# A graph-network stack on TensorE: masks made further ahead, loads less far ahead, and the three-term features moved into the gates' operand tiles

## The chip, the cores and the metric

The kernel runs on one core of one Trainium2 chip. The metric is the device time of one execution in microseconds; the median of three runs is quoted. A profile is one further execution. The engines are TensorE (PE, with its weight loads PEld), VectorE (DVE), ScalarE (ACT), GpSimd (POOL) and SyncE (SP, which issues DMAs). Each engine takes its instructions in the order in which the program holds them.

## What is computed

There are N = 3327 nodes with 64 features each, and one adjacency matrix `adj` (3327 x 3327, float32, some 0.5% of it nonzero). Four layers follow each other, each on the layernorm of the running sum:

```
h = relu(layernorm(x)); x = x + layer(h, adj)
layer 0: two gated cells: m = adj @ (h @ W); gates r, z, n from m and h; h = relu((1-z)*n + z*h)
layer 1: mask = adj != 0; rank = cumsum(mask, axis=1); k = min(deg, 100); pos = rank - (deg - k)
         out = (mask * where(pos > 0, 0.5**(k - pos), 0)) @ (h @ weight) + bias
layer 2: w = adj*adj; three times: h = (w @ h) @ W.T + b
layer 3: two hops: h = tanh(concat(adj @ h, h) @ W)
```

So the adjacency is passed over eight times: twice plain, once with weights by rank (the nonzero entry counted from the end of a row gets a power of one half), three times with squared entries, and twice plain.

## The kernel before

**Tiles and passes.** The transposed, padded adjacency lies in HBM as 26 source blocks of 128 rows. The target nodes are cut into four chunks (`CH`, three of 2 x 384 columns and one of 2 x 512), and these into two groups (`GROUPS`): group 0 is chunks 0 and 1 (768 KB per tile), group 1 is chunks 2 and 3 (896 KB). A `Tile` is one source block for one group. It is loaded into one of 20 slots (`slots`, named adj in the profile) by SP (L368). A unit is (pass k, chunk c, tile): it multiplies the tile's columns of the chunk with the features `y[k]` of the source block and adds to the chunk's sum in PSUM (L561). Passes 0, 1, 6 and 7 are PLAIN, pass 2 is RANKED, passes 3, 4 and 5 are SQUARED.

**The order of units** is written out ahead: `alone(0, 0)`, then `joint(1, 0)`, `joint(0, 1)`, `joint(1, 2)` and so on to `alone(0, 7)`. In `joint(g, k)` each tile of group g serves pass k and pass k + 1, so that the matrix is loaded four and a half times rather than eight. There are 914 units. Units 250 to 313 are pass 2 of group 0, units 314 to 389 pass 2 of group 1, from unit 326 on in turn with units of pass 3.

**The ranked pass.** A unit of pass 2 needs the tile's mask (`Mask`), a bf16 0/1 tile of which half a slot, a room, holds one. `make_mask` puts two pieces, one per half of the columns, into the queue `pieces`. A piece is a compare on DVE (L426); the first piece also issues, on POOL, a DMA of one row of totals into the mask's last row (L431). `run` lets pieces out one by one as units pass (`mask_pieces`); units of pass 2 that belong to group 0 on both sides let none out. What a unit needs is forced out when it is expanded, three units ahead of its own matmuls. `expand` multiplies the mask by a triangular matrix on PE (L270) and turns the two PSUM banks into weights, on ACT (L476) or DVE (L474). Masks of the count (k = -1, in pass 0) are made in the same way without the totals row. For group 0's tiles of pass 2 the mask is made where pass 1 has used the tile (`early`).

**The planner.** For each unit i, `run` first loads tiles up to `LOAD` = 60 units ahead, as long as more than three free slots (`RESERVE`) remain in `dead`. Then it prepares: `prepare` makes masks and squares tiles in place (ACT L403, DVE L405). It goes strictly in the order of the units and stops at the first unit that lies further ahead than its kind allows: 6 units for all kinds but RANKED, 44 for RANKED. So a unit of pass 3 that is more than 6 ahead holds up all masks behind it. Free slots and rooms are handed out first in, first out.

**Tasks between passes.** When a chunk's sum is complete, a generator (`after_0` and so on) evacuates it and computes the next features. Each `yield` names a time; the planner counts that down by the units it puts out and then puts out the next part of the task. If a unit needs features that aren't there, `finish` puts out all that is left of the task. Thus a `yield` decides where a task's instructions stand in each engine's queue. `layernorm_relu` (L761 to L781) computes mean and variance on DVE, the power -0.5 on POOL (L776) and the scaled result on DVE (L780). `gru` (L796 to L840) evacuates into `both` (the gates' operand tiles, two half-filled planes per chunk), computes the gates and, in the first cell, writes relu halves back with ACT (L837) and DVE (L838); L722 then turns these into node rows on PE. `in_three` (L844 to L866) splits the features of pass 2 into three bf16 terms, in one slot per group, and sends the terms' last rows to `lasty` by POOL (L865). The four first layernorms (`before_0`) are put out by a loop at the end, which advances chunks in the order 0, 0, 1, 0, 1, 2, 1, 2, 3, 2, 3, 3.

Of the kernel before, what the change touches and what calls it, by code (L numbers as in the profile page):

```python
# [46 lines left out]
NB = 13  # L47
# [5 lines left out]
NC = 4  # L53
# [18 lines left out]
KIND = [PLAIN, PLAIN, RANKED, SQUARED, SQUARED, SQUARED, PLAIN, PLAIN]  # L72
COUNT = -1
NBUF = 20
LOAD = 60
PREPARE = {COUNT: 6, PLAIN: 6, RANKED: 44, SQUARED: 6}
EXPAND = 3
RESERVE = 3
SPECIAL = None
# [11 lines left out]
def upper(n):  # L91
    return slice(n * D, (n + 1) * D)
# [3 lines left out]
def kernel(  # L96
# [383 lines left out]
            t.mask.free()  # L480
        return wide.bitcast(BF16)

    ranks_left = set(sources_of(*GROUPS[0]))
    counts = {}
    squared = {}

# [46 lines left out]
    def propagate(k, c, t, rhs, first, last):  # L533
        if k == COUNT:
            count(t, first, last)
            return
        w = width(c)
        if first:
            sums[k, c] = [take(sums=True) for _ in range(2 if k == 7 and c == PARTS[1] else 1)]
            sums[k, c] = [sums[k, c][0], sums[k, c][-1]]  # L540
        acc = sums[k, c]
        if t is SPECIAL:
            for ch in range(NC):
                if ch != c:
                    finish(ch)
            terms = [[lasty[:, h, i, :] for h in range(2)] for i in range(3)]
            rhs = [rhs, rhs]
        else:
            s, b = divmod(t.q, NB)
            cs = chunk_of(b)  # L550
            if y[k][cs] is None:
                finish(cs)
            terms = [[yk[:, b - CH[cs][0], s, :]] * 2 for yk in (y[k][cs] if KIND[k] == RANKED else [y[k][cs]])]
            rhs = [rhs[:, h, :] for h in range(2)]
            if KIND[k] != RANKED:
                t.used()
            if (k, c, t) in squared:
                squared.pop((k, c, t)).free()
        for n, yq in enumerate(terms):
            for h in range(2):  # L560
                nc.tensor.matmul(acc[h][1][h * D:(h + 1) * D, :w], yq[h], rhs[h], start=first and n == 0,  # L561
                                 stop=last and n == len(terms) - 1)
        if KIND[k] == RANKED and c == NC - 1 and t is not SPECIAL and chunk_of(t.q % NB) in GROUPS[0]:
            ranks_left.discard(t.q)
            if not ranks_left:
                dead.append(parts[0])
        if t is not SPECIAL and t.early and t.mask is None:
            make_mask(t, RANKED)
        spend(STREAM_US * w / CWM * (0.75 if KIND[k] == RANKED else 1.0))
        if last:  # L570
            begin(c, after[k](c, sums.pop((k, c))))
            if KIND[k] == RANKED and c == NC - 1:
                dead.append(parts[1])

    units = []

# [38 lines left out]
    def joint(g, k, sweep, later, keep, lag=None):  # L615
# [45 lines left out]
        for c in (a, b):  # L661
            for t in own[1]:
                put(k + 1, c, t)
            if KIND[k + 1] == RANKED:
                units.append((k + 1, c, SPECIAL))

    def run():
        total = {}
        for k, c, t in units:
            total[k, c] = total.get((k, c), 0) + 1  # L670
        done = {}
        loaded, prepared, expanded = 0, 0, deque()
        for i, (k, c, t) in enumerate(units):
            while loaded < len(units) and loaded < i + LOAD:
                u = units[loaded][2]
                if u is not SPECIAL and u.slot is None:
                    if len(dead) <= RESERVE and loaded > i + EXPAND:
                        break
                    u.load()
                loaded += 1  # L680
            while prepared < loaded and prepared < i + PREPARE[KIND[units[prepared][0]] if units[prepared][0] != COUNT
                                                               else COUNT]:
                if prepared > i + PREPARE[PLAIN] and not spare and len(dead) <= RESERVE + 1:
                    break
                prepare(*units[prepared])
                prepared += 1
            while len(expanded) < min(EXPAND + 1, len(units) - i):
                assert prepared > i + len(expanded)
                expanded.append(expand(*units[i + len(expanded)]))
            if k != 2:  # L690
                mask_pieces(1 + len(pieces) // 6)
            elif not (c in GROUPS[0] and (t is SPECIAL or chunk_of(t.q % NB) in GROUPS[0])):
                mask_pieces(1)
            n = done[k, c] = done.get((k, c), 0) + 1
            propagate(k, c, t, expanded.popleft(), n == 1, n == total[k, c])
# [65 lines left out]
    def layernorm_relu(h, c, scale=None, pace=1.0, squares_on_scalar=False):  # L761
        n = 2 * blocks(c)
        v = groups(xchunk(c))
        st = work.tile([P, 4, 8], F32, name="st", bufs=4)
        xc = work.tile([P, 8, D], F32, name="t2")
        nc.vector.tensor_reduce(st[:, 0, :n], v, AX.X, ALU.add)
        nc.vector.tensor_scalar(st[:, 1, :n], st[:, 0, :n], 1.0 / D, None, op0=ALU.mult)
        nc.vector.tensor_tensor(xc[:, :n], v, st[:, 1, :n, None].to_broadcast([P, n, D]), ALU.subtract)
        yield 1.5 * pace
        if squares_on_scalar:  # L770
            nc.scalar.activation(groups(h), xc[:, :n], AF.Square)
        else:
            nc.vector.tensor_tensor(groups(h), xc[:, :n], xc[:, :n], ALU.mult)  # L773
        nc.vector.tensor_reduce(st[:, 2, :n], groups(h), AX.X, ALU.add)
        nc.vector.tensor_scalar(st[:, 2, :n], st[:, 2, :n], 1.0 / D, EPS, op0=ALU.mult, op1=ALU.add)  # L775
        nc.gpsimd.tensor_tensor(st[:, 3, :n], st[:, 2, :n], mhalf[:, :n], ALU.pow)  # L776
        yield 2.5 * pace
        if scale is not None:
            nc.vector.tensor_scalar(st[:, 3, :n], st[:, 3, :n], scale, None, op0=ALU.mult)
        nc.vector.scalar_tensor_tensor(groups(h), xc[:, :n], 0.0, st[:, 3, :n, None].to_broadcast([P, n, D]),  # L780
                                       op0=ALU.max, op1=ALU.mult)  # L781
# [14 lines left out]
    def gru(acc, c, bi, bh, cell, pace=1.0):  # L796

        w = width(c)
        evacuate_stacked(acc, c)
        yield 0.8 * pace  # L800
        at = dead.popleft()
        r, z, d = (slots[at].rearrange("p s w -> p (s w)")[:, i * CWM:i * CWM + w] for i in range(3))

        def gate(g):
            i, ps = take()
            for s in range(2):
                nc.tensor.matmul(ps[upper(1 - s), :w], cells[:, cell, s, g, :], both[c][:, s], start=True, stop=True)
            return i, ps

        for g, v in enumerate((r, z)):  # L810
            i, ps = gate(g)
            nc.scalar.activation(v, ps[:, :w], AF.Sigmoid, bias=bsum[:, cell, g:g + 1])
            give(i)
        nh = None if cell == 0 else gate(2)
        ni = gate(3)
        yield 1.0 * pace
        nc.vector.scalar_tensor_tensor(r, ahead[c] if nh is None else nh[1][:, :w], bcol[:, bh + 2:bh + 3], r,
                                       op0=ALU.add, op1=ALU.mult)
        nc.vector.tensor_tensor(r, r, ni[1][:, :w], ALU.add)
        give(ni[0])  # L820
        if nh is not None:
            give(nh[0])
        else:
            del ahead[c]
            if not any(ch in ahead for ch in GROUPS[c // 2]):
                rooms[c // 2].free()
        yield 1.0 * pace
        nc.scalar.activation(r, r, AF.Tanh, bias=bcol[:, bi + 2:bi + 3])
        yield 0.8 * pace
        for s in range(2):  # L830
            u = upper(1 - s)
            nc.vector.tensor_tensor(d[u], both[c][u, s], r[u], ALU.subtract)
        nc.vector.tensor_tensor(d, d, z, ALU.mult)
        nc.vector.tensor_tensor(d, d, r, ALU.add)  # L834
        yield 2.2 * pace
        if cell == 0:
            nc.scalar.activation(both[c][upper(1), 0], d[upper(1)], AF.Relu)  # L837
            nc.vector.tensor_scalar(both[c][upper(0), 1], d[upper(0)], 0.0, None, op0=ALU.max)  # L838
            yield 1.0 * pace
        return at, d  # L840

    parts = {}

    def in_three(h, c):  # L844

        g = c // 2
        if g not in parts:
            parts[g] = dead.popleft()
        n = blocks(c) * 2 * 3 * D
        first = 2 * 3 * D * blocks(GROUPS[g][0]) if c == GROUPS[g][1] else 0  # L850
        room = slots[parts[g]].bitcast(BF16).rearrange("p s w -> p (s w)")[:, first:first + n]
        room = room.rearrange("p (b s i d) -> p b s i d", s=2, i=3, d=D)
        terms = [room[:, :, :, i, :] for i in range(3)]
        for i in range(2):
# [167 lines left out]
```

## Time and profile before

| | us |
|---|---|
| median of 3 runs | 720.03 (719.84 to 720.97) |
| profiled execution | 723.89 |
| its span, first to last instruction | 722.1 |
| PE busy | 690.7 (96%) |
| DVE busy | 346.2 (48%) |
| ACT busy | 264.3 (37%) |
| POOL busy | 77.3 (11%) |
| mean granted clock of PE | 0.993 |
| HBM read | 199.45 MB, 277 GB/s over the span |

The profile is a record of each instruction's start and duration, with what ended the idle time before it. Its views are a page of totals; the busy time per stretch (one row per stretch, one column per engine); the waits (who waited for whom, in total); the chain that ended last; and the timeline, in which instructions of one kind are merged and the idle time before the first stands in brackets. Line numbers are those of the program. Buffers' numbers are left out of names, so that `adj` is any of the 20 slots. The ends of matmuls are modelled, so PE can show as busy where it waits a little between two starts.

### The profile page before, as it was taken

What the parts mean: (1) busy time and instruction counts of PE and PEld (TensorE: products, weight loads), DVE (VectorE), ACT (ScalarE), POOL (GpSimd) and SP (SyncE); (2) the same over time, 40 slices, a digit from 0 to 9 for tenths busy, and PEclk for the clock granted to TensorE, in tenths of its full rate; (3) what the DMA queues carried; (4) which work ended last, traced back from release to release, by engine and by line L of the source; (5) the groups of instructions that cost most, each with busy time, mean ns of one, the idle gap of its engine ahead of it and who ended that gap; (6) DMA issues with size and microseconds to landing.
All of it is one profiled execution on the core that took longest, in us unless ns stands there. A gap on an engine that the chain in (4) does not pass through costs nothing.

```text
span 722.1 us, 12647 instructions
## 1 busy us (share of the span) xinstructions
PE 690.7 (96%) x5128; PEld 347.6 (48%) x5128; DVE 346.2 (48%) x701; ACT 264.3 (37%) x402; POOL 77.3 (11%) x114
## 2 busy tenths in 40 slices
PE   4999899999999897989999999999999999999997
PEld 1645444565446585445534444334444444344464
DVE  6767636634987987638615101521063456005101
ACT  0104000302137665778899321850065700000101
POOL 3500000001380602112100000000010000000000
PEclk9999999999999999999999999999999999999999
DMA  9999994299595367562799829981997399927991
GB/s 349 401 385 406 405 391 145 63 375 374 181 315 210 114 225 237 184 227 97 260 336 386 314 88 397 405 319 40 366 382 263 111 382 406 406 110 250 400 402 44
DMA packets 68549, 201.31 MB, mean 279 GB/s; under 512 B 7228, under 2 KB 8228, under 8 KB 68492
## 3 DMA queue, kind: packets, MB, share of 16 engines
q1 hardware_dynamic: 65596, 199.46, 74.6%
q8 instruction: 40, 0.66, 0.4%
q10 hardware_dynamic: 720, 0.85, 0.3%
q0 software_dynamic: 2176, 0.20, 0.2%
q14 instruction: 17, 0.14, 0.0%
HBM read 199.45 MB, written 0.85 MB: 277 GB/s over the span
## 4 chain that ended last, share of the span: by engine, by line
PE 52%; ACT 4%; DMA 2%; DVE 1%; issue 1%; ACTq 0%
PE sum L561 48%; ACT adj L403 3%; PE temp L270 3%; DMA adj<-totals 1%; PE temp L722 1%; DVE adj L426 1%; DMA out<-xs 1%; DVE both L757 0%; ACT both L756 0%; DVE xs L955 0%; ACT t L701 0%; PE sum L270 0%; ACT t L952 0%; ACT e L476 0%; ACTq L957 0%
## 5 line engine op out<-in xcount | busy, mean ns | idle before, releaser
L561 PE MATMUL sum<-adj,y 128*64 128x384 f32 (+3 forms) x3016 | 535.2, 505 | 12.1 <-DVE y L773 8.4
L561 PEld LDWEIGHTS sum<-adj,y 128*64 128x64 f32 x3016 | 223.3, 138 | 267.5 <-issue 223.8
L403 ACT ACTIVATE adj<-adj 128x768 f32<-128x768 f32 (+1 forms) x173 | 141.9, 891 | 50.2 <-PE sum L561 24.8
L426 DVE TENSOR_SCALAR adj<-adj 128x768 bf16<-128x768 f32 (+3 forms) x208 | 115.6, 606 | 32.4 <-PE temp L496 28.5
L476 ACT ACTIVATE e<-temp,bitsb 128x384 int16<-128x384 f32 (+1 forms) x114 | 65.4, 607 | 29.2 <-PE temp L270 16.1
L561 PE MATMUL sum<-e,adj 128*64 128x384 bf16 (+1 forms) x624 | 73.2, 341 | 0.6 <-DVE e L474 0.6
L757 DVE COPY both<-sum 64x384 f32<-64x384 f32 (+3 forms) x17 | 9.7, 568 | 117.1 <-ACT both L756 116.0
L756 ACT COPY both<-sum 64x384 f32<-64x384 f32 (+3 forms) x17 | 8.1, 478 | 154.8 <-PE sum L561 149.2
L270 PE MATMUL temp<-adj,tri 128*64 128x384 bf16 (+1 forms) x334 | 52.7, 348 | 8.7 <-DMA adj<-totals 5.4
L405 DVE TENSOR_TENSOR adj<-adj 128x768 f32<-128x768 f32 (+1 forms) x35 | 33.6, 1008 | 50.1 <-DMA adj<-in_adjT 29.6
L776 POOL TENSOR_TENSOR st<-st,mhalf 128x6 f32<-128x6 f32 (+1 forms) x16 | 24.5, 1531 | 295.5 <-DVE st L775 295.5
L561 PEld LDWEIGHTS <-adj 128*64 128x64 bf16 x624 | 40.3, 110 | 18.8 <-issue 6.7
L431 POOL DMA_DIRECT2D adj<-totals x52 | 31.4, 605 | 139.8 <-DVE adj L834 74.4
L474 DVE TENSOR_SCALAR e<-temp 128x384 int16<-128x384 f32 (+1 forms) x53 | 31.8, 607 | 26.3 <-issue 11.3
L270 PEld LDWEIGHTS <-tri 128*64 128x64 bf16 x416 | 28.9, 111 | 30.2 <-issue 13.7
L751 DVE STREAM_TRANSPOSE both<-y 32x96 f32<-32x96 f32 (+1 forms) x128 | 35.6, 278 | 2.9
L703 DVE COPY t<-sum 128x384 f32<-128x384 f32 x8 | 4.4, 555 | 62.2 <-PE sum L561 62.2
L496 PE MATMUL temp<-adj,behind 128*64 128x384 bf16 x208 | 29.1, 342 | 0.8 <-DVE adj L426 0.7
L496 PEld LDWEIGHTS <-behind 128*64 128x64 bf16 x208 | 14.1, 112 | 20.8 <-issue 18.6
L701 ACT COPY t<-sum 128x384 f32<-128x384 f32 (+1 forms) x8 | 4.2, 529 | 53.9 <-PE sum L561 53.9
L918 DVE TENSOR_TENSOR y<-temp,brow 128x384 f32<-128x384 f32 (+1 forms) x8 | 4.7, 592 | 29.6 <-PE temp L270 29.6
L530 ACT ACTIVATE lastw<-adj,bitsb 128x768 int16<-128x768 f32 (+1 forms) x2 | 2.0, 984 | 45.8 <-DVE adj L528 45.8
(121 smaller groups left out, 336.7 us busy)
## 6 DMA issues: line engine op xcount, KB each, us to landing
adj<-in_adjT SPq DMA_DIRECT2D x130, 768.0 KB, 8.7
adj<-in_adjT SPq DMA_DIRECT2D x104, 896.0 KB, 12.5
xs<-in_x SPq DMA_DIRECT2D x1, 640.0 KB, 4.0
adj<-totals POOLq DMA_DIRECT2D x26, 3.0 KB, 4.6
adj<-totals POOLq DMA_DIRECT2D x26, 3.5 KB, 3.1
out<-xs ACTq DMA_DIRECT2D x2, 192.0 KB
out<-xs ACTq DMA_DIRECT2D x1, 256.0 KB, 6.4
stage<-in_weights SPq DMA_DIRECT2D x2, 112.0 KB, 13.3
```

The lines of the kernel that those rows point to most:

```text
L270: nc.tensor.matmul(out[hs], lhsT[:, hs], rhs, start=start, stop=stop)
L403: nc.scalar.activation(sq, v, AF.Square)
L405: nc.vector.tensor_tensor(sq, v, v, ALU.mult)
L426: nc.vector.tensor_scalar(t.mask.view[:rows, half], t.view()[:rows, half], 0.0, None, op0=ALU.not_equal)
L431: nc.gpsimd.dma_start(out=t.mask.view[P - 1:P], in_=totals[t.g][t.q:t.q + D + 1:D, :])
L474: nc.vector.tensor_scalar(wide[:, s], ps[:, :w], BITS, 0.0, op0=ALU.add, op1=ALU.max)
L476: nc.scalar.activation(wide[:, s], ps[:, :w], AF.Relu, bias=bitsb)
L496: nc.tensor.matmul(counts[c][1][s * D:(s + 1) * D, :w], behind[:, NQ - 1 - t.q:NQ - 1 - t.q + D], t.mask.view[:, s, t.cols(c)], start=firs ...
L561: nc.tensor.matmul(acc[h][1][h * D:(h + 1) * D, :w], yq[h], rhs[h], start=first and n == 0, stop=last and n == len(terms) - 1)
L751: nc.vector.transpose(to[at:at + 32, :, q], h[q * 32:(q + 1) * 32, :, s, f * 32:(f + 1) * 32])
L757: nc.vector.tensor_copy(both[c][upper(1), 1], acc[1][1][upper(1), :width(c)])
L776: nc.gpsimd.tensor_tensor(st[:, 3, :n], st[:, 2, :n], mhalf[:, :n], ALU.pow)
```

## The change

The planner gets three limits in the place of four. Loads go at most 44 units ahead instead of 60. All kinds are prepared 6 units ahead. Masks of pass 2 that aren't early are made by a loop of their own, up to 24 units ahead, and this loop passes over units of other kinds. Its condition on free slots is the old one. The features of pass 2 (`in_three`) lie in `both` instead of two slots, which therefore stay in `dead`. The layernorm gets one more `yield`, between the last DVE instruction of the variance and the power on POOL, and the one behind the power becomes 1.5 instead of 2.5. In `gru`, the first cell's relu on DVE stands ahead of the yield that it stood behind, and that yield becomes 2.4 instead of 2.2.

```diff
-LOAD = 60
-PREPARE = {COUNT: 6, PLAIN: 6, RANKED: 44, SQUARED: 6}
+LOAD = 44
+PREPARE = 6
+MASK = 24
...
-        if KIND[k] == RANKED and c == NC - 1 and t is not SPECIAL and chunk_of(t.q % NB) in GROUPS[0]:
-            ranks_left.discard(t.q)
-            if not ranks_left:
-                dead.append(parts[0])
...
-            if KIND[k] == RANKED and c == NC - 1:
-                dead.append(parts[1])
...
+    def is_masked(k, c, t):
+
+        return k != COUNT and KIND[k] == RANKED and t is not SPECIAL and not t.early and t.mask is None
+
...
-            while prepared < loaded and prepared < i + PREPARE[KIND[units[prepared][0]] if units[prepared][0] != COUNT
-                                                               else COUNT]:
-                if prepared > i + PREPARE[PLAIN] and not spare and len(dead) <= RESERVE + 1:
-                    break
+            while masked < min(loaded, i + MASK):
+                if is_masked(*units[masked]):
+                    if not spare and len(dead) <= RESERVE + 1:
+                        break
+                    make_mask(units[masked][2], RANKED)
+                masked += 1
+            while prepared < min(loaded, i + PREPARE):
                 prepare(*units[prepared])
                 prepared += 1
...
         nc.vector.tensor_scalar(st[:, 2, :n], st[:, 2, :n], 1.0 / D, EPS, op0=ALU.mult, op1=ALU.add)
+        yield 1.5 * pace
         nc.gpsimd.tensor_tensor(st[:, 3, :n], st[:, 2, :n], mhalf[:, :n], ALU.pow)
-        yield 2.5 * pace
+        yield 1.5 * pace
...
-        yield 2.2 * pace
+        if cell == 0:
+            nc.vector.tensor_scalar(both[c][upper(0), 1], d[upper(0)], 0.0, None, op0=ALU.max)
+        yield 2.4 * pace
         if cell == 0:
             nc.scalar.activation(both[c][upper(1), 0], d[upper(1)], AF.Relu)
-            nc.vector.tensor_scalar(both[c][upper(0), 1], d[upper(0)], 0.0, None, op0=ALU.max)
             yield 1.0 * pace
...
-        g = c // 2
-        if g not in parts:
-            parts[g] = dead.popleft()
-        n = blocks(c) * 2 * 3 * D
-        first = 2 * 3 * D * blocks(GROUPS[g][0]) if c == GROUPS[g][1] else 0
-        room = slots[parts[g]].bitcast(BF16).rearrange("p s w -> p (s w)")[:, first:first + n]
+        room = both[c].bitcast(BF16).rearrange("p s w -> p (s w)")[:, :blocks(c) * 2 * 3 * D]
```

## The prediction

> **What bounds the kernel now.** The first view is the busy time by stage. Columns: stretch and its length in us, then busy us (and instructions) of PE, PEld, DVE, ACT and POOL, granted clock, DMA share, GB/s.
>
> ```profile
> 0.00:20.00 20.00, 10.54 (x49) 4.27 (x50) 14.10 (x30) 1.28 (x1) 9.06 (x18) 1.00 0.93 354
> 230.00:250.00 20.00, 16.62 (x202) 12.27 (x197) 19.55 (x43) 14.14 (x30) 9.92 (x14) 1.00 0.34 118
> 267.00:285.00 18.00, 16.53 (x186) 12.30 (x181) 16.07 (x35) 11.59 (x19) 3.65 (x4) 1.00 0.88 295
> 285.00:295.00 10.00, 6.67 (x46) 3.12 (x46) 4.16 (x8) 3.98 (x6) 0.70 (x2) 0.83 0.09 22
> 317.00:327.00 10.00, 7.95 (x46) 3.16 (x44) 4.59 (x8) 5.08 (x8) 2.92 (x5) 0.83 0.42 146
> ```
>
> TensorE (PE) sets the pace: 690.7 of 722.1 us busy. The change adds and removes no matmul, so all it can win lies in some 31 us of PE idle time and in clock dips. That idle time sits at the start, in 230 to 250 (3.4 us, VectorE full), and round 288 and 320. Next, what PE waited for (total, times, longest):
>
> ```profile
> PE sum L561 <- DVE y L773: 8.4, 1, 8.4
> PE temp L270 <- DMA adj<-totals: 5.4, 2, 3.3
> PE sum L561 <- DMA adj<-in_adjT: 2.8, 5, 1.4
> PE temp L270 <- DVE e L474: 2.3, 3, 1.7
> PE sum L722 <- DVE both L838: 2.1, 1, 2.1
> ```
>
> All five are touched. Last, the timeline round the first and the longest wait for a mask's totals row:
>
> ```profile
> 7.37 0.56 DVE L780 SCALAR_TENSOR_TENSOR y<-t,st 128x384 f32<-128x384 f32 x1 [0.21 <-POOL st L776]
> 8.40 7.35 PE L561 MATMUL sum<-adj,y 128*64 128x384 f32 x32 [8.40 <-DVE y L773]
> ...
> 282.70 1.32 POOL L776 TENSOR_TENSOR st<-st,mhalf 128x6 f32<-128x6 f32 x1 [7.04 <-DVE st L775]
> 283.97 1.19 POOL L431 DMA_DIRECT2D adj<-totals  x2
> 285.13 1.15 DVE L426 TENSOR_SCALAR adj<-adj 127x896 bf16<-127x896 f32 x2
> 288.44 0.52 PE L270 MATMUL temp<-adj,tri 128*64 128x384 bf16 x4 [3.33 <-DMA adj<-totals]
> ```
>
> PE starts 0.47 us after L780 is done. At 288.44 it waits for a row whose DMA was issued at 283.97, behind a power on POOL (L776) that waited for DVE.
>
> **The Trainium skill.** (1) "TensorE: Matmul & The Clock Gate", What's actually happening: the clock is halved after an idle window of about 3.4 us, and windows run freely. The trace agrees in the loss: clock 0.83 in each ten-us stretch above is 1.7 us lost; but waits of 2.1 and 2.05 us were enough, so a window need not be wholly idle, and 1.65 us at 241 cost no clock. (2) "DMA: Bandwidth & Descriptors", Anatomy of one DMA: about 2 us fixed per DMA. Totals rows landed after 1.6 to 5.2 us here, 3.9 to 4.4 round 284. (3) "VectorE: DVE Perf Modes", the TRN2 errata section: 58 + FD/Accel cycles at 0.96 GHz; a mask half of 896 columns at 2x would take 527 ns. Ten back to back took 5.43 us: 0.54; between evictions 0.575. I use 0.56.
>
> **The change, step by step.** Sums are against the profiled execution, 723.89 us (span 722.1, 1.8 round it); the median of the runs is 720.03, 3.86 lower. I take the same microseconds off both. Program order is what the changed program's queues hold.
>
> *1. The layernorm's added yield, at the start.* The loop that interleaves the four first layernorms gives each three turns. With one yield more, all four L780 come after all four first halves on DVE. Before: first L780 at 7.37. Now DVE starts at 3.17 and does three halves of 2.65 (3.17 to 5.82 in the trace) and one of 3.1 (512 columns): 14.2. L780 0.56, then 0.47: PE starts at 15.2, 6.8 later. The cold 3.9 us are paid either way. Part is absorbed, since PE waited for tiles in this stage: from 8.40 to 20.79 it did 6 tiles of 1.29 (8 x 0.161, the pitch of 256 matmuls in 41.28 us), a count of 0.32 and 1.95 of cold loss: 2.4 us of waits. From 20.79 to 40.42, 19.63 for 10 tiles at 1.615 and transposes of 2.8: 0.7. From 40.42 to 57.14, 16.7 for 15.2 of work, at the tiles' pitch of 1.96: 1.5. So 6.8 - 4.6 = **+2.3** (ends +2, and +4.4 if only the first 2.4 is cover). The first chunk's transposes only change place.
>
> *2. The relu L838 ahead of the yield.* Before, it stood behind two mask halves and ended at 76.52; now right behind L834, at 72.7. PE's 2.1 goes. Next late: the count's mask, queued behind both L838, done at 77.1 while PE gets there at 75.5: 1.4 of waiting. The first matmul of pass 1 comes at 80.3 instead of 82.67: **-2.4**, of which 1.7 is the clock dip after the wait. Lower end -0.7 if the new wait still halves the clock.
>
> *3. No slot for the features.* Two of 20 slots stay free; the last six loads of pass 1's group 0 stand 2 to 4 units earlier in SP's queue. The 1.36 wait at 212 to 213.6 mostly goes: **-1.2** (0 to -1.4). The copies and subtractions are as many and as large.
>
> *4. Twelve mask halves leave 233 to 250.* In the program before, six masks of the second group were made here: 12 halves, 6.9 us busy of DVE's 19.55 in 20. They move to after 271. PE stands still for 20 - 16.62 = 3.4 us here, mostly for evictions L474. Without the masks DVE's remaining work (the layernorms and features of two chunks) lets an eviction through every 1.3 us, where PE needs one per two units, 1.6; some tenths stay at the start, where two come 2.3 apart. **-3.0** (-2 to -3.4). Nothing else is late there: ACT is busy 14.14 of 20.
>
> *5. They arrive in 267 to 295.* Chosen and uncertain. Pieces of a mask are not let out while group 0's own units run, so making masks at unit 291 doesn't spread them: in DVE's queue 15 more halves now stand between the pass-2 evacuation (267.43) and the eviction at 291.12. DVE's work there was 23.7 less 5.9 idle = 17.8; plus 15 x 0.56 = 26.2: the eviction at 293.6 at the earliest, +2.5. The totals row still goes out only when the power ahead of it is done; that waits for DVE, so 288.2 instead of 284, landing 1.6 to 4.4 later. PE's matmul of 288.44 then comes at 291.3 to 292.6. Its next 4.6 us were at half clock, 2.9 at full: +1.1 to +2.4 remain, and up to 1 more while DVE has four halves and two evictions (3.3) for PE's 3.39 per cycle. **+2.4** (0 to +5, with two clock dips). So the stall at 285 is not won; it turns into a wait for DVE. Queued behind the masks: evictions, so PE.
>
> *6. The wait at 320.* Four totals rows were issued together at 317.10, after an 8.4 us wait of POOL, and landed in 4.1 to 5.2. Their masks are now made 5 to 15 units earlier, in rooms that other masks have left (a unit takes 0.85 us of PE here): wait 2.05 and dip 1.7: **-3.75** (-2.05 if a dip remains). Next late there is PE itself, which is busy without a gap from 295 to 317.
>
> *7. Loads at most 44 ahead*: 0. Where it bites (pass 7, one to five units later) the three free slots are handed out in the same order, and SP waits for a slot's last reader, not for a unit. The cover is a full DMA queue (share 1.00 and 1.03 from 660 to 700); without it one tile, 2 us. The power's later place on POOL, behind two more totals rows: 0, since L780 comes a yield later too; otherwise 0.54 per row, in step 5's range.
>
> Sum: +2.3 - 2.4 - 1.2 - 3.0 + 2.4 - 3.75 = -5.65: profiled 718.2, median **714.4**.
>
> **Rivals.** *A, masks hidden:* step 5 wins its stall and dip, -5.0: sum -13.05, 707.0. For it: DVE idles 4.3 us between 285 and 291. Against: 26.2 us of DVE work don't fit into the 23.7 - 5.0 = 18.7 that PE would then need. *B, it doesn't do what it says at 320:* rows still late behind POOL's queue, step 6 is 0: 718.1. For it: rooms are reused at once, so a row waits for PE. Against: rooms' waits of 1.4 to 2.9 us, beside leads of 10 us and more. *C, slower, DVE full in 267 to 303:* none of the 15 halves falls in DVE's idle time, 8.6 us at 0.575 on top of the old stall, and one more dip, 1.7: step 5 is +10.3, sum +2.25, 722.3. It decides from a step 5 of +8.05, where the sum is 0. For it: 19.55 of 20 in step 4 shows what a full DVE does to PE. Against: PE's matmuls run three units ahead of their evicted masks.
>
> **How the numbers follow.** Forecast 0.57, A 0.10, B 0.18, C 0.15. The forecast's own range adds its steps' ends as independent: downward 0.3, 0.2, 0.4 and 2.4 give 2.5, upward 2.1, 1.7, 1.2, 1.0, 2.6 and 1.7 give 4.4: 711.9 to 718.8. The range 709.0 to 721.0 leaves out A and most of C. About 0.2% (1.4 us) is what a measurement tells from no change. Faster: 0.54 of the forecast, A, 0.12 of B, 0.76; same: 0.03, 0.05 of B and 0.03 of C, 0.11; slower: 0.01 of B and 0.12 of C, 0.13.
>
> **What would show it.** 1: PE's first matmul at 15.2, pass 0's first evacuation 2.3 later. 2: no wait for the relu; a wait on L496. 3: no wait for a tile round 212. 4: PE 19.5 or more of 20 in 230 to 250. 5: DVE near full for 25 us from the first evacuation of pass 2. 6: no totals wait in the second half of pass 2. A start that costs all of 6.8, or a row's wait of over 4 us, would make the prediction wrong.

## The result, and the profile after

The changed kernel takes 721.02 us (median of 12 runs, 720.38 to 723.35); the kernel before, beside it, 720.64 (12 runs, 718.12 to 723.38). The ratio is 1.000, 95% interval 0.9988 to 1.0013: no change that can be measured. The profiled execution took 720.42 us with a span of 718.2.

So two numbers have to be explained. Profile against profile, the change won 3.85 us of the 5.65 forecast. Run against run it won nothing.

Where the profiles part is read from events that both have: the start of the same evacuation or eviction in each.

| event | before | after | difference | step | its share | forecast |
|---|---|---|---|---|---|---|
| pass 0, first evacuation | 59.67 | 61.29 | +1.62 | 1, start | +1.62 | +2.3 |
| pass 0, third evacuation | 130.97 | 130.26 | -0.71 | 2, relu | -2.33 | -2.4 |
| pass 1, third evacuation | 214.51 | 212.29 | -2.22 | 3, slot | -1.51 | -1.2 |
| pass 2, first evacuation | 267.43 | 261.31 | -6.12 | 4, masks leave | -3.90 | -3.0 |
| evictions from 294 on | 297.37 | 298.81 | +1.44 | 5, masks arrive | **+7.56** | **+2.4** |
| pass 2, third evacuation | 346.09 | 342.24 | -3.85 | 6, rows at 320 | -5.29 | -3.75 |

From there to the end the difference stays -3.85. The first evacuation of pass 2, before and then after, as the timeline of DVE has them:

```profile
267.43 0.55 DVE L703 COPY t<-sum 128x384 f32<-128x384 f32 x1
```

```profile
261.31 0.55 DVE L704 COPY t<-sum 128x384 f32<-128x384 f32 x1
```

The stages of the kernel after, with the columns as in the prediction:

```profile
0.00:20.00 20.00, 4.99 (x30) 2.89 (x32) 15.42 (x32) 2.23 (x3) 10.51 (x19) 1.00 0.92 351
...
230.00:250.00 20.00, 19.78 (x238) 15.46 (x236) 16.55 (x37) 16.24 (x33) 7.84 (x12) 1.00 0.72 264
...
267.00:285.00 18.00, 11.51 (x100) 6.68 (x98) 14.06 (x29) 5.78 (x10) 4.14 (x5) 0.88 0.20 64
285.00:295.00 10.00, 9.11 (x76) 5.05 (x72) 9.24 (x18) 7.09 (x10) 5.89 (x8) 0.87 0.02 4
...
317.00:327.00 10.00, 10.00 (x80) 4.87 (x78) 4.30 (x8) 8.65 (x15) 1.61 (x3) 1.00 0.79 268
```

In the first row PE has half of its former work, since it starts at 15 us. The second and the last row show what was won: PE 19.78 of 20 and 10.00 of 10. The price stands in 267 to 285, where PE was busy 16.53 of 18 before and now 11.51, with the clock down. And VectorE isn't full there: 14.06 of 18. What PE waited for (total, times, longest):

```profile
PE temp L740 <- DVE y L782: 15.0, 1, 15.0
PE temp L271 <- DVE adj L427: 5.7, 6, 1.7
PE sum L271 <- DVE adj L427: 3.1, 3, 2.1
...
PE sum L561 <- DMA adj<-in_adjT: 0.7, 1, 0.7
```

The relu's wait and the rows' waits are gone; 8.8 us of waits for mask halves (L427) are new. The timeline of PE and of DVE from 263 to 272 shows how such a wait comes about:

```profile
265.15 0.56 DVE L769 TENSOR_TENSOR t<-xs,st 128x384 f32<-128x384 f32 x1
265.62 1.16 DVE L427 TENSOR_SCALAR adj<-adj 127x896 bf16<-127x896 f32 x2
267.22 0.56 DVE L475 TENSOR_SCALAR e<-temp 128x384 int16<-128x384 f32 x1 [0.44 <-PE temp L271]
269.06 0.69 DVE L475 TENSOR_SCALAR e<-sum 128x512 int16<-128x512 f32 x1 [1.29 <-PE sum L271]
269.67 0.55 DVE L774 TENSOR_TENSOR y<-t 128x384 f32<-128x384 f32 x1
270.26 0.55 DVE L775 TENSOR_REDUCE st<-y 128x6 f32<-128x384 f32 x1
270.84 0.17 DVE L776 TENSOR_SCALAR st<-st 128x6 f32<-128x6 f32 x1
270.92 1.16 DVE L427 TENSOR_SCALAR adj<-adj 127x896 bf16<-127x896 f32 x2
```

```profile
266.29 0.35 PE L271 MATMUL sum<-adj,tri 128*64 128x384 bf16 x2 [2.12 <-DVE adj L427]
...
268.69 1.23 PE L561 MATMUL sum<-e,both 128*64 128x384 bf16 x6
271.60 0.35 PE L271 MATMUL temp<-adj,tri 128*64 128x384 bf16 x2 [1.68 <-DVE adj L427]
```

At 269.06 DVE has idled 1.29 us for a matmul; then it does an eviction and three layernorm steps, and only then the two halves for which PE is waiting since 269.9. Each engine waits for the other in turn, and neither is full.

### The profile page after: what moved, and what is told of

Its sections match the earlier page's. It is cut to its first block, busy times and chain, and to the rows that moved or that the text cites. A ratio compares the mean times of both kernels' runs of the same rounds, so it can differ in the third digit from the quotient of the medians.

```text
span 718.2 us, 12625 instructions
## 1 busy us (share of the span) xinstructions
PE 685.5 (95%) x5128; PEld 354.0 (49%) x5128; DVE 343.5 (48%) x700; ACT 264.4 (37%) x403; POOL 79.2 (11%) x114
## 4 chain that ended last, share of the span: by engine, by line
PE 54%; ACT 4%; issue 1%; DVE 0%; ACTq 0%
PE sum L561 50%; ACT adj L404 4%; PE temp L271 3%; PE temp L723 1%; DVE both L758 0%; ACT both L757 0%; ACT t L702 0%; DVE xs L951 0%; PE sum L271 0%; ACTq L953 0%; ACT t L948 0%; ACTq L404 0%; ACT e L477 0%; ACTq L757 0%; ACTq L948 0%
## 5 line engine op out<-in xcount | busy, mean ns | idle before, releaser
L561 PEld LDWEIGHTS sum<-adj,y 128*64 128x64 f32 x3016 | 228.6, 137 | 248.9 <-issue 222.7
L427 DVE TENSOR_SCALAR adj<-adj 128x768 bf16<-128x768 f32 (+3 forms) x208 | 113.1, 594 | 37.8 <-PE temp L496 33.9
L561 PE MATMUL sum<-e,both 128*64 128x384 bf16 (+1 forms) x624 | 74.6, 347 | 0.0
L561 PEld LDWEIGHTS <-both 128*64 128x64 bf16 x624 | 40.8, 112 | 19.3 <-issue 6.6
L475 DVE TENSOR_SCALAR e<-temp 128x384 int16<-128x384 f32 (+1 forms) x53 | 32.2, 609 | 22.4 <-PE temp L271 10.7
L496 PEld LDWEIGHTS <-behind 128*64 128x64 bf16 x208 | 16.8, 110 | 17.7 <-issue 16.5
L271 PE MATMUL sum<-adj,tri 128*64 128x384 bf16 (+1 forms) x82 | 15.5, 342 | 3.2 <-DVE adj L427 3.1
```

The lines of the kernel that those rows point to most:

```text
L271: nc.tensor.matmul(out[hs], lhsT[:, hs], rhs, start=start, stop=stop)
L427: nc.vector.tensor_scalar(t.mask.view[:rows, half], t.view()[:rows, half], 0.0, None, op0=ALU.not_equal)
L475: nc.vector.tensor_scalar(wide[:, s], ps[:, :w], BITS, 0.0, op0=ALU.add, op1=ALU.max)
L496: nc.tensor.matmul(counts[c][1][s * D:(s + 1) * D, :w], behind[:, NQ - 1 - t.q:NQ - 1 - t.q + D], t.mask.view[:, s, t.cols(c)], start=firs ...
```

## The experiments

Twelve versions, each with its runs of the kernel before beside it. Where a version is compared with the changed kernel's 721.02, the two weren't measured side by side; the medians of the kernel before beside them lie within 0.4 us of each other (720.24 to 720.64). "Half clock" is the share of the span lost to it, (1 - granted clock) x span, as a mean over the runs; for the changed kernel it is 4.13 us.

| version | median us (runs) | before | ratio, 95% interval | half clock, us |
|---|---|---|---|---|
| before_again | 721.08 (14) | 720.53 | 0.9993 (0.9975 to 1.0012) | 2.78 (119 runs: 2.58, see below) |
| after_start | 718.96 (19) | 720.53 | 0.9975 (0.9962 to 0.9988) | 3.93 |
| after_pieces | 717.12 (6) | 720.53 | 0.9946 (0.9925 to 0.9966) | 0.12 |
| after_both | 715.23 (6) | 720.53 | 0.9915 (0.9896 to 0.9933) | 0.36 |
| before_relu | 719.63 (14) | 720.24 | 0.9988 (0.9974 to 1.0003) | 2.41 |
| before_three | 717.03 (11) | 720.24 | 0.9954 (0.9937 to 0.9972) | 1.30 |
| before_plan | 726.62 (6) | 720.24 | 1.0087 (1.0063 to 1.0111) | 5.32 |
| after_mask44 | 718.08 (19) | 720.24 | 0.9963 (0.9950 to 0.9976) | 0.34 |
| after_oldln | 724.63 (13) | 720.55 | 1.0044 (1.0023 to 1.0066) | 5.11 |
| before_yield | 721.35 (22) | 720.55 | 1.0023 (1.0003 to 1.0043) | 2.00 |
| both_mask30 | 715.43 (8) | 720.55 | 0.9930 (0.9903 to 0.9956) | 0.27 |
| both_mask34 | 712.93 (6) | 720.55 | 0.9895 (0.9864 to 0.9927) | 0.47 |

### before_again: was the profiled execution of before a usual one?

> The kernel before, unchanged, for a second profiled execution of it. Its first one took 723.89 us with a span of 722.1, while twelve timed runs of it have a median of 720.64 (718.12 to 723.38). Theory A: that profiled execution was a late one, with stalls or half-clock stretches that most executions lack; this one then has a span near 719 and at most one half-clock stretch before 330 us in place of three (at 77, 289 and 323). Theory B: executions differ in the launch only; this span is near 722 again, with the same three stretches at the same places. Timed: 720.6, ratio 1.00 under both.

Its profiled execution has a span of 718.1, 4.0 less than the first one, with the same program. Theory A holds. The first stretch in the first profile of before (the two others stand in the prediction), and all three in this one:

```profile
60.00:100.00 40.00, 37.71 (x260) 18.97 (x258) 23.24 (x45) 7.78 (x14) 0.74 (x1) 0.96 1.03 406
```

```profile
60.00:100.00 40.00, 37.71 (x268) 18.69 (x266) 24.20 (x46) 7.88 (x14) 0.74 (x1) 1.00 1.03 405
285.00:295.00 10.00, 8.62 (x57) 3.96 (x58) 4.84 (x9) 5.78 (x8) 1.07 (x2) 0.83 0.21 67
317.00:327.00 10.00, 8.27 (x74) 4.12 (x70) 5.38 (x10) 6.52 (x12) 2.16 (x5) 1.00 0.53 171
```

The relu's wait is there in both and as long (2.13 us), but only in the first execution half clock follows it: 0.96 against 1.00 in 60 to 100. At 320 it is the same (0.83 against 1.00), and the row's wait itself is 1.73 instead of 2.05. Only the stretch round 288 is at half clock in both.

All 119 runs of the kernel before beside these versions (with before_again's own) bear this out: median 720.49, 717.24 to 725.65, half clock 2.58 us in the mean. A straight line through them gives span = 715.7 + 1.22 x half clock, correlation 0.90. The profiled execution of before that the forecast started from had lost 5.1; 11 of the 119 runs (9%) lost as much.

Against this second profile the changed kernel's profile is 0.1 us longer (718.2 against 718.1), which is what the medians say. Step 2 then wins 1.70 us, the rows at 320 win 1.92 (3.94 against the first), and step 5 costs 8.45.

### after_start: the order of the first layernorms

```diff
-        yield 1.5 * pace
+        if split:
+            yield 1.5 * pace
...
-    yield from layernorm_relu(h, c)
+    yield from layernorm_relu(h, c, split=False)
```

(`split` is false in `before_0` alone; then the pause after the power is 2.5 again.)

> The changed kernel, with the layernorm's steps as before in the four layernorms ahead of pass 0 alone (one pause of 2.5 after the power). Theory (the added pause turns the order on VectorE from chunk by chunk to step by step, and costs PE 1.62 us that the tile waits don't absorb): PE's first matmul at 8.4 again, span 1.6 shorter than the changed kernel's 718.2, timed 719.4. Rival (DMA paces the first 60 us, so the start is worth nothing; the 1.62 came from elsewhere): 721.0 as the changed kernel.

2.1 us less than the changed kernel, where 1.6 was expected: by the runs the theory holds, and the start is worth 1.6 us or a little more, though PE starts 6 us earlier. This version's own profile doesn't show it. Its first matmul comes at 8.84, held by a tile in the end, not by L782, but the first evacuation of pass 0 comes at 61.11, only 0.18 earlier than in the changed kernel. It is an exception: in the nine other profiles with the old start this evacuation comes at 59.6 to 60.2, in the four with the new one at 61.3 to 62.2, some 2 us later.

### after_pieces: the same halves, let out earlier

```diff
-            elif not (c in GROUPS[0] and (t is SPECIAL or chunk_of(t.q % NB) in GROUPS[0])):
+            else:
                 mask_pieces(1)
```

> The changed kernel, with mask halves let out one a unit in all units of pass 2, also those in which the first group works on its own sources (there none came out but those due at once). No work is added or removed. In the changed kernel 5 halves of the second group's masks come out only when due and 17 more just ahead, between the first evacuation of pass 2 at 261 and 293 us, where PE waits 9 us for VectorE's halves and runs 6.8 us at half clock although VectorE is busy only 14.1 of 18 us. Theory A (order: each late half makes PE wait for a VectorE step that itself waits in line behind an eviction, which waits for PE): with 15 halves out in the twenty units before, these waits fall to 2 us or less and the half-clock stretches go; span about 709, timed about 712. Theory B (VectorE is short of time there whatever the order): waits move to 250 to 267 us, and the time stays within 1.5 us of 721.0.

3.9 us less than the changed kernel, no half clock left. So the order counts, but not alone: theory A gave 712, and 717.1 came out. The stretches 250 to 267 and 267 to 285 of this version:

```profile
250.00:267.00 17.00, 13.99 (x151) 9.86 (x146) 17.00 (x34) 9.20 (x16) 3.26 (x5) 1.00 0.45 142
267.00:285.00 18.00, 15.27 (x164) 11.04 (x166) 16.61 (x35) 10.75 (x17) 4.20 (x5) 1.00 0.39 130
```

Now VectorE is full in 250 to 267 (17.00 of 17), and the first evacuation of pass 2 comes at 266.35 instead of 261.31: 5 us are lost there, 9 won behind it, of which 3.4 are the two stretches at half clock. Theory B has its part: in these 17 us there is too little of VectorE's time.

### after_both: the two edits together

The edits of after_start and after_pieces, as above.

> The two edits together: the start's layernorms as before, and mask halves let out in all units of pass 2. If both theories hold and the stretches lie apart (0 to 60 us, and 250 to 300 us), the sum: timed about 710.5, 1.6 below the version with the halves alone. If neither holds, 721.0. If only the start counts, 719.4.

715.23: 1.9 less than with the halves alone. The two add up; the 710.5 failed only by what after_pieces had failed by.

### before_relu, before_three, before_plan, before_yield: each part alone

```diff
# before_relu
-        yield 2.2 * pace
         if cell == 0:
-            nc.scalar.activation(both[c][upper(1), 0], d[upper(1)], AF.Relu)
             nc.vector.tensor_scalar(both[c][upper(0), 1], d[upper(0)], 0.0, None, op0=ALU.max)
+        yield 2.4 * pace
+        if cell == 0:
+            nc.scalar.activation(both[c][upper(1), 0], d[upper(1)], AF.Relu)
```

> The kernel before, with the relu of VectorE issued ahead of the pause and the pause of 2.4 after it (as the change has it), and nothing else. Theory: PE's wait of 2.13 us for it at 74 us, the same in both profiled executions of the kernel before, goes, and 0.5 of it comes back as a wait for the counting mask behind it: 1.6 to 2.1 us faster, timed 718.8. The half-clock stretch at 77 us that my prediction added to it (1.7 us) stood in one of two executions, so on the average it adds some 0.8 more at most. Rival (the next tile or mask is late anyway, so that the wait only changes its name): 720.6.

The wait went from 2.13 to 0.52 us (for the count's mask). The time, 0.6 us less by the medians, can't be told from no change. The traces show where the gain goes. Against the profile of before_again, this one is 1.4 us earlier at pass 0's third evacuation (129.02), 0.9 earlier at pass 1's third, where PE waits 1.37 us for a tile instead of 0.85, and even at the evictions from 294 on, since the row's wait at 286 is 3.34 instead of 2.31. So a later wait for a tile and one for a row take most of it in this execution; that they do so in most executions isn't shown.

before_three takes the diff's part on `in_three`, `parts` and `ranks_left`, and nothing else:

```diff
-            parts[g] = dead.popleft()
...
-        room = slots[parts[g]].bitcast(BF16).rearrange("p s w -> p (s w)")[:, first:first + n]
+        room = both[c].bitcast(BF16).rearrange("p s w -> p (s w)")[:, :blocks(c) * 2 * 3 * D]
```

> The kernel before, with the three-term features put into the place of the gates' operands, so that they take no slot, and nothing else. Theory (a slot more for tiles at 180 to 220 us takes away PE's wait for a tile at 212, 1.36 and 0.85 us in two executions): 1 us faster, timed 719.6. Rival (loads there are held by bandwidth, not by slots): 720.6.

3.2 us less, three times the forecast. PE has no wait for a tile round 212, and the row's wait at 319 is 0.67 instead of 1.73 or 2.05. Half clock falls from 2.58 to 1.30 us, so about half of the gain is clock, by the straight line above. (Its profiled execution, 719.21, is the slowest of its runs.)

before_plan takes the diff's constants, `is_masked` and `run`, and nothing else:

```diff
-LOAD = 60
-PREPARE = {COUNT: 6, PLAIN: 6, RANKED: 44, SQUARED: 6}
+LOAD = 44
+PREPARE = 6
+MASK = 24
```

> The kernel before, with the planner's part of the change alone: loads at most 44 units ahead, masks up to 24 units ahead past units of other passes, other preparation 6 ahead. Theory: it is the part that costs. It wins the 3.4 us of PE's idle time at 233 to 250 and the waits for the totals' rows at 284 and 319 (2.3 to 3.3 and 1.7 to 2.1), and loses 9 us of waits for late mask halves at 264 to 293 and one or two half-clock stretches (1.7 us each): from 1 us slower to even, timed 721.2, and clock lower than before's. Rival (the waits of 264 to 293 come from the layernorm's second pause or the slots freed, not from the planner): the gains alone, 4 us or more faster, 716.5.

6.4 us slower, five more than expected. The rival is refuted: the planner's part is what costs. Its longest waits aren't those of the changed kernel, though:

```profile
PE temp L271 <- DMA adj<-totals: 7.8, 2, 5.0
PE sum L271 <- DVE adj L427: 2.9, 2, 2.1
PE temp L271 <- DVE adj L427: 2.9, 4, 1.5
```

Here PE waits 7.8 us for totals' rows, which the changed kernel doesn't. What takes these waits away is another part of the change; after_oldln shows which. before_yield is the layernorm's added pause alone:

```diff
+        yield 1.5 * pace
         nc.gpsimd.tensor_tensor(st[:, 3, :n], st[:, 2, :n], mhalf[:, :n], ALU.pow)
-        yield 2.5 * pace
+        yield 1.5 * pace
```

> The kernel before with the layernorm's added pause alone. Theory: the start costs 1.6 us; the wait of 2.3 to 3.4 us for a totals' row at 284, which stood behind the power on GpSimd, goes with about one half-clock stretch, since the power now comes a pause later: timed 718.5, with a clock of 0.998 or better. Rival (the row only changes place with the power and lands no earlier): the start's cost alone, 722.1.

0.8 us slower by the medians. The rival is nearer: the waits for rows stay (2.5 and 2.2 us), so alone the pause costs the start, and half clock shrinks only from 2.58 to 2.00.

### after_oldln: the change without the layernorm's pause

```diff
-        yield 1.5 * pace
         nc.gpsimd.tensor_tensor(st[:, 3, :n], st[:, 2, :n], mhalf[:, :n], ALU.pow)
-        yield 1.5 * pace
+        yield 2.5 * pace
```

> The changed kernel with the layernorm's pauses as before everywhere (the power directly behind the variance, then one pause of 2.5); all else as changed. It tells what the added pause does in pass 2. Theory (the planner's part needs it: with the power ahead of the totals' rows in GpSimd's order, PE waits for these rows 5.0 and 2.8 us, as in the kernel before with the planner's part alone, 726.6): the start wins 1.6 and pass 2 loses 5 or more, timed 724. Rival (the power's place in pass 2 is worth nothing, as my prediction's last step had it): only the start's gain, 719.4.

724.63, as the theory had it. GpSimd's timeline in the changed kernel, and then without the pause:

```profile
246.49 1.12 POOL L432 DMA_DIRECT2D adj<-totals  x2
271.17 1.58 POOL L778 TENSOR_TENSOR st<-st,mhalf 128x6 f32<-128x6 f32 x1 [23.57 <-DVE st L776]
272.73 2.59 POOL L432 DMA_DIRECT2D adj<-totals  x4
```

```profile
245.56 0.59 POOL L432 DMA_DIRECT2D adj<-totals  x1 [0.33 <-PE temp L271]
271.24 1.58 POOL L777 TENSOR_TENSOR st<-st,mhalf 128x6 f32<-128x6 f32 x1 [25.09 <-DVE st L776]
272.80 2.21 POOL L432 DMA_DIRECT2D adj<-totals  x4
```

And PE's in the version without the pause:

```profile
274.50 0.53 PE L271 MATMUL temp<-adj,tri 128*64 128x384 bf16 x2 [4.57 <-DMA adj<-totals]
```

GpSimd stands for 24 us at the power, which waits for VectorE. With the pause one more row stands ahead of the power in its queue (x2 against x1 at 246) and is issued 26 us earlier. Without it, PE waits 4.57 us for that row.

### after_mask44, both_mask30, both_mask34: how far ahead

after_mask44 is the changed kernel with 44; the two others are after_both with 30 and with 34.

```diff
-MASK = 24
+MASK = 44
```

> The changed kernel with masks up to 44 units ahead in place of 24. Then the second group's first 14 halves come out 20 units sooner, at 240 to 250 us, as in the kernel before, and none only when due. Theory (the depth of 24 is what put the halves late): the waits of 264 to 293 us and their half-clock stretches shrink to 3 us or less, PE's idle 3.4 us at 233 to 250 comes back, net 3 to 5 us faster than the changed kernel, timed 717. Rival (the waits come with VectorE's load in pass 2, whenever the halves come): 721.

718.08, 2.9 us less. The halves come out at 240 to 250, and PE idles 3.7 us in 230 to 250 again:

```profile
230.00:250.00 20.00, 16.32 (x197) 12.01 (x194) 19.59 (x44) 14.25 (x29) 9.75 (x13) 1.00 0.77 287
```

No wait for L427 is left in pass 2. Waits for evictions (L475) are, 5 us behind 264, more than the 3 expected. So the depth of 24 did put the halves late; the depth of 44 brings back the stretch at 230 to 250 in which VectorE is full (19.59 of 20).

> The version with the start's layernorms as before and halves let out in all units of pass 2, with masks up to 30 units ahead in place of 24. In it VectorE was busy 17.0 of 17 us in 250 to 267 and PE lost 4.7 us there, while VectorE had 2.5 us free in 240 to 250. Now 5 halves (2.9 us) come out there. Theory (what is left is VectorE's time in that stretch): 2 to 3 us faster than 715.2, timed 713. Rival (the loss is a chain of order, not of time): 715.2.

715.43: nothing won, as the rival had it. PE lost less of 250 to 267 (14.35 busy, against 13.95 in after_both), but also waited for evictions in 267 to 285 (14.12 busy, against 15.20). VectorE is full in 250 to 267 in both.

> As the version with 30, with masks up to 34 units ahead: 9 halves (5.2 us) come out before 250 us, more than VectorE has free there (2.5 us). Theory (VectorE's time): as the one with 30 or up to 1 us slower, since PE then waits in 240 to 250: 713 to 714. Rival (the earlier the better): 712.

712.93, the best version and 1.05% faster than the kernel before. VectorE's own stretches:

```profile
240.00:250.00 10.00, 9.84 (x104) 6.70 (x102) 9.75 (x20) 7.34 (x16) 8.84 (x13) 1.00 0.18 64
250.00:267.00 17.00, 15.41 (x176) 11.67 (x175) 17.00 (x34) 9.41 (x16) 1.81 (x3) 1.00 0.34 111
267.00:285.00 18.00, 15.33 (x158) 10.48 (x156) 17.12 (x37) 11.21 (x18) 4.46 (x5) 1.00 0.32 104
```

PE has 1.4 us more of work in 250 to 267 than in after_both, and loses 0.1 in 240 to 250 for it, although VectorE is nearly full there. That 30 gives none of this and 34 does wasn't foreseen by either theory; that halves fall at other evictions is a guess, and this stays open. Nor do the profiles put all of it there: of the 2.4 us between the spans of after_both (713.5) and this version (711.0), 1.2 are there already at pass 0's third evacuation, ahead of pass 2; after_both waits 1.40 us for a tile just before it.

## Why the prediction was wrong, point by point

**The base: a chance taken for a property.** Two terms of the forecast failed, the base and step 5. The sum counted three stretches at half clock, 1.7 us each, as something that the kernel before always has: in step 2 (1.7 of its 2.4), in step 6 (1.7 of its 3.75) and in step 5's base. And it carried the profile to the median with a fixed 3.86 us. Both failed. The profiled execution of before lost 5.1 us to half clock, its runs 2.58 in the mean; it was 3.4 us above the median of the 119. Nor did the 3.86 pass over: the changed kernel's profiled execution, 720.42, lies 0.6 below its median. Of the 6.64 us between 714.38 and 721.02, this is 3.86 + 0.60 = 4.46; the other 2.18 lie between the profiles (718.24 forecast, 720.42 measured; 1.8 in the steps, the rest outside the span).

How often half clock follows a wait can be estimated. The windows lie on a fixed grid of 3.41 us: in the first profile of before the three stretches start at 77.3, 288.9 and 323.0, which is 62.0 and 10.0 windows apart. In the fourteen profiles of this case, leaving out the first 20 and the last 15 us, 15 windows in which PE idled for 2.05 us or more (60%) were followed by one at half clock, one of 2.05 was not, and none of 1.98 or less was, save where the clock was already halved. The Trainium skill, "TensorE: Matmul & The Clock Gate", What's actually happening, calls the window free-running, and these runs agree: in the ten profiles with the old start the clock is full from 3.6 to 5.8 us behind PE's first matmul on, not at one fixed distance from it. So a wait of 2.13 us brings half clock only if nearly all of it falls into one window: (3.41 - 2.13 + 2 x 0.08) / 3.41 = 0.42 of all starts, an estimate. In the same way the rows' waits of 3.33 and 2.05 give 0.77 and 0.40. In sum 1.59 stretches of 1.7 us: 2.7 us, where the runs show 2.58 (some 0.3 of them behind the last matmuls, by the profiles). All three in one execution, as in that profile, would be one in eight if they were independent, which isn't shown; 9% of the runs lost that much.

**Step 5, mis-sized: +7.56 for +2.4.** Among the steps this is the term that failed. The prediction counted VectorE's work ("26.2: the eviction at 293.6 at the earliest"), took VectorE to do it without idle time, and PE to be three units ahead of it. The work was counted rightly; that VectorE would have no idle time in it is what failed. From the first evacuation of pass 2 to that eviction (291.12 before, 292.85 after), before and then after:

```profile
267.43:291.12 23.69, 18.89 (x196) 13.31 (x194) 17.48 (x38) 13.31 (x21) 3.81 (x4) 0.95 0.67 225
```

```profile
261.31:292.85 31.54, 22.51 (x198) 13.35 (x194) 26.00 (x53) 13.37 (x21) 9.85 (x13) 0.89 0.27 89
```

VectorE is busy 26.00 us, but the stretch takes 31.54: 5.5 us of idle time that the sum had at nothing. What counted was order. Five halves came out only when due and seventeen just ahead of it, behind layernorm steps and behind evictions that waited for PE: 8.8 us of waits, and two stretches at half clock, 3.4; in the kernel before, one wait of 3.33 and one stretch of 1.7 stood there. after_pieces takes away the half clock and the waits for halves with the same work, against 5 us of waits for evictions; after_mask44 takes away all waits for halves. Rival C had a full VectorE and +10.3; it named the right place and the wrong cause. That order isn't all is seen in after_pieces, where VectorE is full.

**Step 7's last sentence, "The power's later place on POOL, behind two more totals rows: 0".** Wrong by about 5 us, in the change's favour. With the pause out, the changed kernel is 3.6 us slower (724.63 against 721.02), although the start then wins 1.6. The step saw rows moving ahead of the power as a cost of 0.54 each; the gain is that a row no longer waits for VectorE. In the sum this is part of step 5, which would have been worse without it.

**Right in mechanism and nearly in size.** Step 1: PE's first matmul at 15.01 (15.2 forecast), +1.62 left of it for +2.3 (some 2 over the profiles). Step 2: the relu's wait gone, 0.5 us behind it for 1.4, -2.33 for -2.4; against the second profile of before, which has no half clock there, -1.70. Step 3: no wait at 212, -1.51 for -1.2. Step 4: PE 19.78 of 20, -3.90 for -3.0, beyond its end of -3.4. Step 6: no row's wait, -3.95, as forecast; 1.35 more came at 336 to 343, where the kernel before let five mask halves out only when due and the changed one a single one. Step 7's loads: nothing lost, since the difference is -3.85 from 346 us to the end; no run has this limit alone. The rows, which it took to land after 5.2 us at most, landed after up to 6.5. Rival B, that rows stay late at 320, fell; so did A. That the profiles' forecast missed by no more than 2.18 is luck in part: step 5 costs 5.16 more than forecast, while the start costs 0.68 less and steps 3, 4 and 6 win 2.75 more.

**What the parts are worth together.** Alone, by the ratios: relu -0.12%, features -0.46%, planner +0.87%, pause +0.23%; in sum +0.52%, 3.7 us slower. Together they are even. The missing 3.7 us come from the pause and the planner's part needing each other: without the pause the three other parts give +0.44% together (after_oldln) and +0.29% in the sum of their own, so it is the pause, +0.23% alone, that is worth -0.44% beside them.

## What to carry to other kernels

Take more than one profiled execution before costing a change against one, and count a half-clock stretch by the share of executions that have it. When work is moved to a place where an engine has idle time, ask when each piece is due and what it stands behind: pieces that come out only when due cost their consumer a round trip each, though no engine is full. A queue that mixes DMA issues with arithmetic holds each DMA until the arithmetic ahead of it has its operand; one place in that queue made PE wait 4.6 us here.

## What the runs showed of the hardware

The clock is halved after windows that aren't wholly idle: 2.05 us of idle time in one window of 3.41 us was the border: of 16 windows with as much or more, 15 were followed by one at half clock. The same wait of 2.13 us brought half clock where 2.13 of it fell into one window (before), and none where 1.98 did (before_again). So a shorter wait can be worth more than its length: versions whose waits in pass 2 all stay under 2 us (after_pieces, after_both, after_mask44, both_mask30, both_mask34) lose 0.1 to 0.5 us to half clock where the kernel before loses 2.58, and in their profiles no stretch between start and end is at half clock. The 19 runs of after_mask44 lie within 1.7 us of each other, where the 37 of the kernel before beside them spread over 6.7.
